# One bank for a block's own keys in the row maxima of a causal attention

## The chip, the core and the metric

The kernel runs on one core of a Trainium2 chip. The metric is the device time of one launch in microseconds (us). A profiled execution comes with it: its span runs from the first to the last instruction, and a little time lies around the span.

The engines are named as the profile names them: PE is the matrix engine (PEld its weight loads, which overlap its products), DVE the vector engine, ACT the scalar engine, POOL the general one, SP the one that issues the DMAs here. PE's results go to PSUM, in banks of 512 fp32 columns by 128 partitions.

## The reference

Four layers follow each other on x (4 batches, 1024 rows, 256 features) with a context of 77 rows a batch. The change is in layer 0, a causal self-attention that also sees the context, then a feed-forward part:

```python
q, k_self, v_self = ...            # 16 heads of 16
k = jnp.concatenate([k_self, k_ctx], axis=1)
scores = jnp.einsum('bthd,bshd->bhts', q, k) * scale
mask = (j >= t) | (j <= i)         # context keys always, own keys up to the row
attn = jax.nn.softmax(jnp.where(mask, scores, -jnp.inf), axis=-1)
x = x + attn @ v
x = x + gelu(ln(ln(x)) @ w1 + b1) @ w2 + b2
```

Layer 1 joins a linear attention to the context with a window attention of 64 rows; layers 2 and 3 are attentions to the context alone.

## The kernel before

**Units.** Layer 0 goes over units: a batch and a block of four heads ("quad"), 16 units in all. A unit's queries and keys lie transposed in one tile, each head in its own 32 partitions, so that the products of the four heads run in four row groups of PE side by side. The keys are ordered with the 77 of the context first, then the 1024 of the sequence: query tile t (128 rows, t = 0 to 7) sees columns 0 to 77 + 128 t + 128, and of the last 128 of them, its own keys, only the lower triangle. Tiles 0 to 3 are block 0, tiles 4 to 7 block 1.

**Two passes.** First the row maxima of the scores are taken (class `Max0`, line 562): queries stand, keys stream, DVE reduces the bank in PSUM to one value for each row and head (line 601), into `mpart`, which has three places for each query tile, head and block. When a block is complete, one small reduce over the places gives the negated maximum (line 609), which PE transposes and DVE adds into a spare row of the queries (`maxima_into`, line 521). Then the scores are computed once more, transposed, keys standing (`Sum0`, line 630); ACT takes the exponential out of PSUM (line 666), and PE multiplies it with the values (`sums`).

**The causal mask.** In the maxima's pass the mask is a product: the identity (bf16) stands, a tile `maskd` with 0 and -1e30 streams, and the product is added into the bank behind the keys' products (lines 587 to 592). `maskd` is made by POOL at the start (lines 205, 227, 228) and is two query tiles wide. A bank that ends one query tile's keys gets 128 columns of it, a bank that ends two gets 256, which are put where the own keys lie.

**Banks and plan.** A bank holds up to 512 columns of scores of a head; `MAX0` (line 620) is the plan written out by hand: eleven banks for a unit, each a list of (query tile, place in `mpart`, first key, last key). The fifth closes block 0, the eleventh block 1.

**Bursts.** `step` (line 485) pairs the eleven banks of a unit with the twelve banks of weights of the unit before (`weights0`; block 0 first). Each pair gives two bursts: two heads of the one beside the other two heads of the other. `burst` (line 471) writes the products in rounds: the maxima's first product for both heads, the weights' first for both heads, the maxima's second, and so on; behind the burst come the reduce and the exponential. A burst takes two buffers of two banks each from a pool of two such buffers (`pair_tile`, line 482), so that its products wait until DVE and ACT have read the burst before. Whichever of the two is taken first goes to the maxima. A PE product in fp32 stands in the profile as two passes, each with its weight load.

**Filler.** Between the bursts `step` puts the weighted sums of the bank before last (only behind the second burst of a pair) and pieces of jobs: projections, feed-forward, preparation of the later layers (`gap`, line 455). A burst's share of the jobs is worked out from the widest bank in it (`cols`). The order of every engine's instructions is thus fixed in the program.

Of the kernel before, what the change touches and what calls it, by code (L numbers as in the profile page):

```python
# [12 lines left out]
BF16 = mybir.dt.bfloat16  # L13
AF = mybir.ActivationFunctionType
ALU = mybir.AluOpType
AX = mybir.AxisListType

P = 128
NB, T, D, S = 4, 1024, 256, 77
# [12 lines left out]
def tile_xattn_seq(ctx: ExitStack, tc: tile.TileContext, d: dict, out: bass.AP):  # L32
    nc = tc.nc
# [5 lines left out]
    work = first.enter_context(tc.tile_pool(name="work", bufs=2))  # L39
# [99 lines left out]
    def clear(qk):  # L139
        nc.gpsimd.memset(qk, 0.0)  # L140
        nc.scalar.activation(qk[:, 1, :], qk[:, 1, :], AF.Identity, bias=onecol, scale=1.0)
# [60 lines left out]


    identb = cpool.tile([P, P], BF16, name="identb")
    maskd = work.tile([P, 2, P], BF16, name="maskd", tag="maskd", bufs=1)
    maskw = work.tile([P, 2, P + WIN], BF16, name="maskw", tag="maskw", bufs=1)
    maskw2 = work.tile([P, 2, P + WIN], BF16, name="maskw2", tag="maskw2", bufs=1)

# [7 lines left out]
    mpart = [work.tile([P, 4, 4, 3], F32, name=f"mpart{i}", tag=f"mpart{i}", bufs=1) for i in range(2)]  # L216
# [4 lines left out]
    def first_constants():  # L221
        clear(qks[0])
        for m in mpart:
            nc.gpsimd.memset(m, NEG)
        nc.gpsimd.tensor_copy(identb, ident)

        nc.gpsimd.memset(maskd, 0.0)
        nc.gpsimd.affine_select(
            out=maskd, in_=maskd, compare_op=ALU.is_ge, fill=NEG, base=0,
            pattern=[[0, 2], [-1, P]], channel_multiplier=1,  # L230
        )
        for m in mrow:
            nc.gpsimd.memset(m, 0.0)
        for v in (vas[0], vcs[0], vas[1], vcs[1]):
            nc.gpsimd.memset(v, 1.0)
# [197 lines left out]
    def defer(gaps, fn):  # L433
        later.append([gaps, fn])

    class Job:


        def __init__(self, gen, n, a=0.0, b=1.0, rest=False):
            self.gen, self.n, self.a, self.b, self.did, self.rest = gen, n, a, b, 0, rest  # L440
# [77 lines left out]
    def rows_of(j):  # L518
        return slice(HP * j, HP * j + HP)

    def maxima_into(qT, q0, m):

        pm = sm.tile([P, 4, P], F32, name="pm", tag="sm")
        for i in range(4):
            nc.tensor.transpose(pm[:, i, :], m[:, i, :], ident)  # L525
        qs = qT[:, q0 : q0 + 512]
        nc.vector.tensor_tensor(qs, pm.rearrange("p i n -> p (i n)"), qs, ALU.add)  # L527

    def extra_of(m):

        return m.rearrange("p i (j r) -> p i j r", r=HP)[:, :, :, DH]
# [30 lines left out]
    class Max0:  # L562

        def __init__(self, u, segs, last):
            self.u, self.segs, self.last = u, segs, last
            self.cols = sum(k1 - k0 for _, _, k0, k1 in segs)

        def matmuls(self, p, ps):  # L570
            u = self.u
            heads = tuple(enumerate((2 * p, 2 * p + 1)))
            rounds, ends, o = [], [], 0
            for t, _, k0, k1 in self.segs:
                qs = slice(P * t, P * t + P)
                rounds.append([
                    ((ps[:, i, o : o + k1 - k0], u["qT"][rows_of(j), qs],
                      u["kT"][rows_of(j), k0:k1]), dict(start=(o == 0), stop=True))
                    for i, j in heads
                ])  # L580
                o += k1 - k0
                if k1 == S + P * t + P:
                    ends.append(o)
            if ends:

                n = len(ends)
                far = ends[-1] - ends[0] if n > 1 else P
                a = ends[0] - P
                rounds.append([
                    ((ps[:, i, a : a + n * far].rearrange("p (k n) -> p k n", k=n)[:, :, 0:P],  # L590
                      identb, maskd[:, 0:n]), dict(start=False, stop=True))
                    for i in range(2)
                ])
            return rounds

        def take(self, p, ps):
            o = 0
            for t, ci, k0, k1 in self.segs:
                bl, i = divmod(t, 4)
                w = k1 - k0  # L600
                nc.vector.tensor_reduce(  # L601
                    mpart[bl][:, i, 2 * p : 2 * p + 2, ci], ps[:, :, o : o + w],
                    axis=AX.X, op=ALU.max,
                )
                o += w
            if self.last is not None and p:
                u, bl = self.u, self.last
                m = mrow[bl]
                nc.vector.tensor_reduce(
                    extra_of(m), mpart[bl], axis=AX.X, op=ALU.max, negate=True  # L610
                )

                def into():
                    maxima_into(u["qT"], 512 * bl, m)
                    u["maxed"].add(bl)

                defer(1, into)


    MAX0 = (  # L620
# [4 lines left out]
    )  # L625

    def maxima0(u):
        return [Max0(u, segs, {4: 0, 10: 1}.get(i)) for i, segs in enumerate(MAX0)]

# [992 lines left out]

    run(stats0(0))
    first_constants()
    head_masks()
    next(keep("c00", lambda: context0(0)))
# [5 lines left out]
    for b in range(NB):  # L1632
        for quad in range(4):
# [12 lines left out]
            u = units[0, b, quad]  # L1646
# [3 lines left out]
    for b in range(NB):  # L1650
        for quad in range(4):
            u = units[1, b, quad]
# [96 lines left out]
```

## Time and profile before

| | us |
|---|---|
| median of 3 runs (2474.48 to 2475.53) | 2475.52 |
| profiled execution | 2472.59 |
| its span | 2470.9 |
| layer 0, paired units, about 112 to 1200 us of the span: PE busy | 988.07 of 1088 |
| in the same stretch: DVE, ACT, POOL busy | 593.14, 440.44, 178.56 |
| all products of layer 0's and 1's scores on PE (`ps<-qk`, with some mask products) | 616.5, 5760 records |
| reduces of the maxima on DVE (line 601), 448 | 409.0 |
| exponentials of layer 0 on ACT (line 666), 384 | 363.2 |

The granted clock of PE is 0.97 of full in layer 0 and 0.99 behind it. In the rows of the profile, L45 is the line of the helper that writes every product, so products are told apart by their tiles: `ps<-qk` are keys' products, `ps<-maskd,identb` the mask. "32x461 f32" is the moving operand, 32 partitions by 461 columns; a merged row names one of the shapes in it.

### The profile page before, as it was taken

To read this page: it belongs to the slowest core of one execution; us is meant where nothing else is said; L and a number is where in the kernel's file an instruction comes from. 1 tells how busy PE (TensorE), PEld (TensorE's weight loads), DVE (VectorE), ACT (ScalarE), POOL (GpSimd) and SP (SyncE) were. 2 spreads that over 40 slices of the span, in tenths; PEclk is the share of its full clock that TensorE was granted. 3 is DMA by queue.
4 is the path that set the end of the run, shared out by engine and by line. 5 is a ranking of instruction groups with operands and counts; after the bars stand their busy time and mean duration, and the time that the engine had idled before them with its cause. 6 is when DMAs were issued, how large, how long until landed. Compare 5 with 4: busy or idle time off the path is not lost.

```text
span 2470.9 us, 39772 instructions
## 1 busy us (share of the span) xinstructions
PE 2284.0 (92%) x16162; PEld 1376.6 (56%) x16162; DVE 1398.5 (57%) x2347; ACT 1033.3 (42%) x1716; POOL 640.5 (26%) x923
## 2 busy tenths in 40 slices
PE   5789989898998989989999999999997999899999
PEld 3433434344444544445456766666654777788887
DVE  4446456654466444665436345454436899776664
ACT  1244344344344334433453343444444677532222
POOL 2011013111131111311134223333341366643222
PEclk9699999999999999999999999999998999999999
DMA  6402021100000000010000100111104334022200
GB/s 176 115 25 93 6 72 41 45 6 14 1 6 15 6 14 2 5 35 5 14 6 14 19 16 15 19 19 19 19 1 151 124 120 133 28 52 57 54 14 18
DMA packets 87136, 98.49 MB, mean 40 GB/s; under 512 B 31222, under 2 KB 77866, under 8 KB 86826
## 3 DMA queue, kind: packets, MB, share of 16 engines
q1 hardware_dynamic: 86954, 95.95, 14.5%
q8 instruction: 128, 2.10, 0.4%
q14 instruction: 54, 0.44, 0.1%
HBM read 57.70 MB, written 20.59 MB: 32 GB/s over the span
## 4 chain that ended last, share of the span: by engine, by line
PE 78%; DVE 11%; ACT 6%; issue 2%; POOL 1%; DMA 1%; SPq 1%; ACTq 0%; DVEq 0%; POOLq 0%
PE ps L45 33%; PE po L45 15%; PE pp L45 6%; PE pv L45 5%; DVE mpart L601 5%; PE ph L45 4%; PE ppv L45 2%; PE psT L1285 2%; PE pvw L45 2%; ACT pe L666 2%; PE ptx L338 1%; PE pvl L45 1%; PE pk L45 1%; PE pt L542 1%; PE pm L525 1%
## 5 line engine op out<-in xcount | busy, mean ns | idle before, releaser
L45 PE MATMUL ps<-qk 32*128 32x192 f32 (+8 forms) x5760 | 616.5, 468 | 102.1 <-DVE mpart L601 54.4
L666 ACT ACTIVATE pe<-ps 128x1024 f32<-128x1024 f32 (+2 forms) x384 | 363.2, 952 | 612.2 <-PE ps L45 607.0
L601 DVE TENSOR_REDUCE mpart<-ps 128x2 f32<-128x1024 f32 (+3 forms) x448 | 409.0, 933 | 349.1 <-PE ps L45 348.7
L45 PEld LDWEIGHTS ps<-qk 32*128 32x128 f32 (+1 forms) x5760 | 288.2, 185 | 375.0 <-DVE mpart L601 134.1
L45 PE MATMUL po<-U,pT 128*128 128x256 f32 (+1 forms) x1280 | 290.5, 382 | 7.4 <-DVE x L1405 4.7
L45 PEld LDWEIGHTS po<-U,pT 128*128 128x128 f32 (+1 forms) x1280 | 239.8, 191 | 50.0 <-ACT pT L1286 8.0
L669 POOL TENSOR_SCALAR_AFFINE_SELECT pe<-pe 128x256 f32<-128x256 f32 (+1 forms) x192 | 95.0, 495 | 637.0 <-ACT pe L666 636.1
L1056 DVE TENSOR_REDUCE mrow<-ps 128x4 f32<-128x768 f32 x128 | 122.5, 957 | 141.4 <-PE ps L45 141.0
L1286 ACT COPY pT<-psT 128x512 f32<-128x512 f32 (+1 forms) x192 | 92.0, 517 | 228.1 <-PE psT L1285 228.0
L1131 ACT ACTIVATE pew<-ps 128x768 f32<-128x768 f32 x128 | 103.4, 811 | 173.4 <-PE ps L45 172.6
L1136 POOL TENSOR_SCALAR_AFFINE_SELECT pew<-pew 128x512 f32<-128x512 f32 x128 | 81.6, 637 | 342.0 <-ACT pew L1131 342.0
L45 PE MATMUL pv<-pe,va 128*32 128x512 f32 (+3 forms) x1536 | 165.0, 518 | 0.1
L45 PE MATMUL ps<-G,xT 128*128 128x308 f32 x512 | 143.0, 423 | 0.0
L45 PE MATMUL ph<-yT,w 128*128 128x256 f32 x512 | 138.1, 405 | 0.8 <-DVE qk L527 0.8
L1366 ACT ACTIVATE s<-s,nm 128x77 f32<-128x77 f32 x512 | 131.2, 352 | 15.9 <-DVE nm L1399 15.9
L1498 POOL TENSOR_TENSOR s<-s,den 128x1232 f32<-128x1232 f32 x32 | 72.0, 2249 | 207.7 <-DVE den L1497 192.4
L45 PEld LDWEIGHTS ph<-yT,w 128*128 128x128 f32 x512 | 93.6, 198 | 52.6 <-issue 39.1
L45 PE MATMUL po<-w,hT 128*128 128x256 f32 x512 | 117.0, 382 | 0.0
L45 PEld LDWEIGHTS ps<-G,xT 128*128 128x128 f32 x512 | 92.4, 190 | 26.8
L45 PEld LDWEIGHTS po<-w,hT 128*128 128x128 f32 x512 | 95.4, 190 | 21.0 <-issue 9.1
L527 DVE TENSOR_TENSOR qk<-pm,qk 128x512 f32<-128x512 f32 x64 | 44.0, 688 | 105.2 <-PE pm L525 105.2
L818 DVE TENSOR_SCALAR hT<-ph,c_L_xattn_b 128x256 f32<-128x256 f32 x128 | 61.3, 480 | 72.4 <-PE ph L45 65.2
(191 smaller groups left out, 3175.7 us busy)
## 6 DMA issues: line engine op xcount, KB each, us to landing
side<-in_fside_t SPq DMA_DIRECT2D x32, 616.0 KB
qk<-st SPq DMA_DIRECT2D x256, 64.0 KB
U<-kept_u SPq DMA_DIRECT2D x8, 1152.0 KB
side<-in_mask_t SPq DMA_DIRECT2D x32, 154.0 KB
G<-kept_g SPq DMA_DIRECT2D x4, 1232.0 KB
x<-in_x SPq DMA_DIRECT2D x8, 512.0 KB
out<-x SPq DMA_DIRECT2D x32, 128.0 KB
kept_u<-st SPq DMA_DIRECT2D x21, 154.0 KB
```

The lines of the kernel that those rows point to most:

```text
L45: nc.tensor.matmul(o, lhsT, rhs, start=start, stop=stop, **kw)
L601: nc.vector.tensor_reduce(mpart[bl][:, i, 2 * p : 2 * p + 2, ci], ps[:, :, o : o + w], axis=AX.X, op=ALU.max,)
L666: nc.scalar.activation(pp[:n, :, o:512], ps[:n, :, o:512], AF.Exp, scale=SC)
L669: nc.gpsimd.affine_select(out=own, in_=own, compare_op=ALU.is_ge, fill=0.0, base=0, pattern=[[0, 2], [0, k], [1, P]], channel_multiplier=-1,)
L818: nc.vector.tensor_scalar(h[:, f, :], ph, cols["L0_xattn_b1"][:, 4 * half + f : 4 * half + f + 1], None, ALU.add,)
L1056: nc.vector.tensor_reduce(mo, ps.rearrange("p j (i n) -> p j i n", i=2)[:, :, :, 0 : P + WIN], axis=AX.X, op=ALU.max, negate=True,)
L1131: nc.scalar.activation(pp[:, :, :, 0 : P + WIN], ps.rearrange("p j (i n) -> p j i n", i=2)[:, :, :, 0 : P + WIN], AF.Exp, scale=SC,)
L1136: nc.gpsimd.affine_select(out=pf[:, :, 0:P], in_=pf[:, :, 0:P], compare_op=ALU.is_ge, fill=0.0, base=0, pattern=[[0, 4], [1, P]], channel_ ...
L1285: nc.tensor.transpose(ps[:, k, :], s[:, P * c : P * c + P], ident)
L1286: nc.scalar.copy(pT[:, 4 * group : 4 * group + n, :], ps[:, 0:n, :])
L1366: nc.scalar.activation(hs, hs, AF.Exp, bias=p1["nm"][:, h : h + 1], scale=SC)
L1498: nc.gpsimd.tensor_tensor(s3, s3, den.unsqueeze(2).to_broadcast([P, H, S]), ALU.mult)
```

## The change

The own keys of the four query tiles of a block are put together in one bank: four products of 128 columns a head, one behind the other, and over them one mask product of 512 columns. `maskd` becomes four query tiles wide. There are two such banks in a unit, named 0 and 1 in the plan, the second and the seventh. The keys in front of the own ones fill the nine other banks, which have no mask any more. The own bank is reduced by one instruction for its four query tiles, into place 0 of `mpart`.

```diff
-    maskd = work.tile([P, 2, P], BF16, name="maskd", tag="maskd", bufs=1)
+    maskd = work.tile([P, 4, P], BF16, name="maskd", tag="maskd", bufs=1)
...
-            pattern=[[0, 2], [-1, P]], channel_multiplier=1,
+            pattern=[[0, 4], [-1, P]], channel_multiplier=1,
...
         def __init__(self, u, segs, last):
-            self.u, self.segs, self.last = u, segs, last
-            self.cols = sum(k1 - k0 for _, _, k0, k1 in segs)
+            self.u, self.segs, self.last, self.own = u, segs, last, None
+            if isinstance(segs, int):
+                self.own = segs
+                self.segs = [
+                    (t, 0, S + P * t, S + P * t + P) for t in range(4 * segs, 4 * segs + 4)
+                ]
+            self.cols = sum(k1 - k0 for _, _, k0, k1 in self.segs)
...
-                if k1 == S + P * t + P:
-                    ends.append(o)
-            if ends:
-
-                n = len(ends)
-                far = ends[-1] - ends[0] if n > 1 else P
-                a = ends[0] - P
+            if self.own is not None:
                 rounds.append([
-                    ((ps[:, i, a : a + n * far].rearrange("p (k n) -> p k n", k=n)[:, :, 0:P],
-                      identb, maskd[:, 0:n]), dict(start=False, stop=True))
+                    ((ps[:, i], identb, maskd.rearrange("p k n -> p (k n)")),
+                     dict(start=False, stop=True))
                     for i in range(2)
                 ])
...
         def take(self, p, ps):
             o = 0
-            for t, ci, k0, k1 in self.segs:
+            if self.own is not None:
+                nc.vector.tensor_reduce(
+                    mpart[self.own][:, :, 2 * p : 2 * p + 2, 0].rearrange("p t j -> p j t"),
+                    ps.rearrange("p j (t n) -> p j t n", n=P), axis=AX.X, op=ALU.max,
+                )
+            for t, ci, k0, k1 in self.segs if self.own is None else ():
...
     MAX0 = (
-        ((3, 0, 0, 461),), ((2, 0, 0, 461),), ((1, 0, 0, 333), (7, 2, 973, 1101)),
-        ((0, 0, 0, 205), (4, 1, 512, 717)), ((5, 1, 512, 845), (3, 1, 461, 589)),
-        ((6, 1, 461, 973),), ((7, 0, 0, 461),), ((7, 1, 461, 973),), ((5, 0, 0, 512),),
-        ((4, 0, 0, 512),), ((6, 0, 0, 461),),
+        ((3, 1, 0, 461),), 0, ((2, 1, 0, 333), (0, 1, 0, 77)), ((6, 1, 512, 845), (4, 1, 512, 589)),
+        ((1, 1, 0, 205), (5, 1, 512, 717)), ((7, 1, 512, 973),), 1, ((7, 2, 0, 512),),
+        ((5, 2, 0, 512),), ((4, 2, 0, 512),), ((6, 2, 0, 512),),
     )
```

In the compiled program the keys' products of the maxima go from 56 to 80 a unit, the mask products from 20 to 8, and the reduces stay at 28.

More of the change, by code (lines that the diff above doesn't have):

```diff
@@ L572, in matmuls @@
             heads = tuple(enumerate((2 * p, 2 * p + 1)))
-            rounds, ends, o = [], [], 0
+            rounds, o = [], 0
             for t, _, k0, k1 in self.segs:
```

## The prediction, made before the changed kernel ran

> **What bounds the kernel now.** I read the page first, for the share of the engines and the chain that ended last; then the stages, by windows; then, inside layer 0, what PE waits for; last the timeline of PE, burst by burst, because the change only reshapes bursts.
>
> ```profile
> span 2470.9 us, 39772 instructions
> ...
> PE 2284.0 (92%) x16162; PEld 1376.6 (56%) x16162; DVE 1398.5 (57%) x2347; ACT 1033.3 (42%) x1716; POOL 640.5 (26%) x923
> ...
> PE 78%; DVE 11%; ACT 6%; issue 2%; POOL 1%; DMA 1%; SPq 1%; ACTq 0%; DVEq 0%; POOLq 0%
> ```
>
> PE carries 78% of the chain and is busy 92%. The windows and PE's waits inside layer 0 say the same of the stage that is changed:
>
> ```profile
> 112.00:1200.00 1088.00, 988.07 (x6964) 464.47 (x6956) 593.14 (x981) 440.44 (x510) 178.56 (x298) 0.97 0.09 24
> ```
>
> ```profile
> PE ps L45 <- DVE mpart L601: 53.1, 80, 1.3
> ...
> PE ps L45 <- ACT pe L666: 15.1, 26, 0.9
> ```
>
> Between 112 and 1200 us PE works 988 of 1088 us; what it does wait for is mostly the reduce of the maxima, whose bank the next burst needs. So time taken from PE's bursts comes back nearly one to one, and the same holds where the reduce is the gate, because the mask stands ahead of the reduce. The masks themselves, shapes kept apart:
>
> ```profile
> L45 PE MATMUL ps<-maskd,identb 128*128 128x256 bf16 x192 | 37.7, 281 | 0.0
> L45 PE MATMUL ps<-maskd,identb 128*128 128x128 bf16 x128 | 18.5, 231 | 0.0
> ```
>
> That is 56 us for all 320, the most that could be at stake. Now the timeline of PE. Its second column is the length of a merged row; the step from one row's start to the next one's is what a piece costs.
>
> ```profile
> 569.62 1.14 PE L45 MATMUL ps<-qk 32*128 32x512 f32 x8
> 570.69 1.98 PE L45 MATMUL pp<-xT,wqk 128*128 128x512 f32 x4
> ```
>
> ```profile
> 612.03 1.37 PE L45 MATMUL ps<-qk 32*128 32x461 f32 x8 [0.52 <-ACT pe L666]
> 613.34 0.29 PE L45 MATMUL ps<-maskd,identb 128*128 128x128 bf16 x2
> 613.55 1.06 PE L45 MATMUL pv<-pe,vc 77*32 77x512 f32 x8
> 614.55 1.42 PE L45 MATMUL ps<-qk 32*128 32x333 f32 x16
> 615.90 0.39 PE L45 MATMUL ps<-maskd,identb 128*128 128x256 bf16 x2
> ```
>
> ```profile
> 1200.55 1.10 PE L45 MATMUL ps<-qk 32*128 32x64 f32 x16
> 1201.58 0.50 PE L45 MATMUL ps<-maskw,identb 128*128 128x384 bf16 x2
> ...
> 1508.43 0.50 PE L45 MATMUL ps<-maskw,identb 128*128 128x384 bf16 x2
> 1508.86 1.06 PE L45 MATMUL pvl<-pel,vc 77*32 77x512 f32 x8
> ```
>
> To be seen: a burst of four 512-column products, each in its own 32 rows and each recorded as two passes, takes 1.07 us. The pair of masks adds 0.21 us at 128 columns (613.34 to 613.55) and 0.43 at 384 (1508.43 to 1508.86) when a product in 32-column tiles follows; at 256 columns with a full-array product behind, 0.23 (the next row starts at 616.13). So a pair costs 0.107 us per 128 columns plus a fixed part: about 0.10 us before a tiled product, about 0.015 before a full-array one. That fixed part, not the columns, is what the change can save.
>
> **The masks.** A unit is one block of four heads; there are 16, and units 1 to 15 pair each bank of maxima with a bank of weights. For each pair of heads the old plan has masks over 1, 2, 2, 2 and 1 own tiles in five bursts, eight tiles in all; the new has four and four in two bursts, also eight. The columns cancel. Three pairs go per head pair, two head pairs, 15 units: 90 pairs. In the second burst of a bank the weighted sums, tiled, always follow: 45 x 0.10 = 4.5 to 4.9 us. In the first burst comes filler: of the 45 old 256-column pairs there the timeline shows 27 followed by a full-array product, 8 by a tiled one, 10 by PE waiting. For these last the reduce starts 0.62 us after the burst's last pass starts when there is no mask, 0.84 with 128 columns: the fixed part is 0.22 - 0.107 = 0.115. So 27 x 0.015 + 18 x 0.11 = 2.4 us. Together -7.0 us; the ends are -5.2 (all first bursts at 0.015) and -9.9 (all at 0.11).
>
> **The own banks.** Instead of one product of 461 or 512 columns a head they run four of 128, each with two passes and its own weight load, while the weights' 512 columns run in the other two row groups. That is 24 products and 48 loads more a unit. The columns are no more than before, so the question is whether loads keep up. The trace's single records give it: in the burst at 1200.55 (64, 128 and 192 columns in turn beside 512) the loads of one row group start 109, 112, 112 and 111 ns apart, and a 128-column pass after a 333-column one (614.55) follows the former pass by 112 ns. 128 columns of a pass take 107 ns ((384 - 104)/333 = 0.84 ns a column, 104 ns until the first pass streams). So eight passes: 104 + 107 + 6 x 112 + 107 + 88 ns of ending = 1.08 us against 1.07: +0.013 us x 60 bursts = +0.8 us.
>
> [...] In the burst at 1200.55 the 128-column pass, issued behind the 512-column product, starts at 0.271, before that product's second pass at 0.505, and the burst takes 1.03 us to the mask (1201.58). [...]
>
> If the 512-column product of the burst has to wait for its bank (ACT or DVE), the own tiles behind it wait as well. They then need 6 x 112 + 195 ns = 0.87 us, less than the 1.02 of the product they stand behind: nothing is added.
>
> **The other key bursts.** 333 + 77 in place of 333 + 128 beside 384 + 128: 1.095 becomes about 1.08 (without a mask the nearest row, 461 beside 384 + 128, takes 1.08), -0.015 x 30 = -0.5 us. 205 + 205 beside 256 becomes 333 + 77 beside 256, and 333 + 128 beside 512 becomes 205 + 205 beside 512: in most of them the second product waits for its bank 0.3 to 0.5 us, then runs its own 0.65 or 1.02 us; the same before and after, 0. The rest are 512 beside 512 or less.
>
> **DVE, ACT, POOL, SP.** Still 14 reduces a head pair, over the same columns (a reduce costs 1224 ns at 1024 elements, 852 at 666, 416 at 256: near enough a line), so 0; five bursts change by about 0.1 us up or down and cancel. The bank of own keys is reduced in one instruction of the 1024-element size. The last bank of each block stays in its place (fifth and eleventh), so the transposition of the maxima and the weights behind it keep their turn. The due times of the filler follow each burst's widest bank, 512 or 410 as before, so no job, no DMA on SP and no eviction is moved in units 1 to 15. Building the wider mask on POOL costs some 0.3 us at 16 us (0.31 + 0.42 us now), while the first burst runs at 39.9 us: hidden by 20 us and more. Unit 0 has no weights beside it: three groups of four masks fewer at about 0.1 us, eight more loads a burst: 0.
>
> Sum: -7.0 + 0.8 - 0.5 = -6.7 us. The profiled execution was 2472.6 us (span 2470.9 and 1.7 around it), 2.9 below the median of the runs; the same 6.7 off the median 2475.5 gives 2468.8, say 2469.
>
> **Rivals.** (a) The reduce is the gate almost everywhere, so each lost pair frees 0.115: -10.4, 2464 to 2465. For it speak 53 us of waits for the reduce, against it that PE idles only some 9% of the layer. [...] (c) Slower: loads throttle the own banks. In the three-tile burst one 128-column pass follows another by 165 ns (0.271 to 0.436), though the loads were 112 apart. If all six spacings were 165, an own burst would last 1.40 us: +0.325 x 60 = 19.5, less 7.5, is +12: 2487. It breaks even at about 132 ns and is slower by over 5 us from 145.
>
> **Numbers.** A measurement of this kernel can tell about 0.2%, 5 us, from no change. The forecast, 2465.5 to 2473, has 0.50; (a) 0.12; (b) 0.22; (c) 0.16. Faster by over 5 us: 0.35 of the forecast and all of (a), 0.47. Slower: (c) and a little of (b), 0.18. The rest, 0.35, within. Range: from the full mask bound less the second-order gain, 2462, to just short of (c)'s whole price, 2484.
>
> **What would show it.** 128 mask products of 512 columns in place of 320, a pair taking 0.44 us before full-array and 0.54 before tiled products; own bursts of 1.08 us before their mask (1.26: program order holds; 1.4: loads); reduce time of the maxima the same; PE idle in layer 0 near 100 us as before. I am wrong if the own bursts exceed 1.2 us, or if PE's wait for DVE or ACT grows by what its busy time loses.

## The result and the profile after

| | before | after |
|---|---|---|
| median of 7 runs (lowest to highest), us | 2474.01 (2471.02 to 2475.53) | 2466.58 (2463.03 to 2472.39) |
| profiled execution; its span, us | 2472.59; 2470.9 | 2470.36; 2468.7 |

The ratio after to before is 0.9973, with 95% interval 0.9962 to 0.9985. The forecast was 2469.0, range 2462 to 2484. What follows shows that the number is nearer the mark than its terms: of the 7.4 us between these medians the step-for-step comparison below gives about 3 to the change.

Page and window of the changed kernel:

```profile
span 2468.7 us, 40924 instructions
...
PE 2273.2 (92%) x16738; PEld 1410.7 (57%) x16738; DVE 1399.1 (57%) x2347; ACT 1032.1 (42%) x1716; POOL 640.1 (26%) x923
...
PE 77%; DVE 11%; ACT 6%; issue 2%; POOL 1%; DMA 1%; SPq 1%; ACTq 0%; DVEq 0%; POOLq 0%
```

```profile
112.00:1200.00 1088.00, 978.54 (x7575) 499.34 (x7572) 598.80 (x989) 443.38 (x516) 178.88 (x299) 0.97 0.10 24
```

PE's busy time in layer 0 went from 988.07 to 978.54 us, 9.5 less, while the span lost only 2.2. PE's waits from 112 to 1190 us say where some of it went:

```profile
PE ps L45 <- DVE mpart L606: 54.2, 83, 1.3
PE ps L45 <- ACT pe L671: 22.1, 30, 1.6
...
PE ps L45 <- DVE mpart L599: 2.8, 14, 0.2
```

Lines 606 and 599 are the reduces (599 that of the own bank), 671 the exponential. The wait for DVE went from 53.1 to 54.2 + 2.8, that for ACT from 15.1 to 22.1: together 11 us more of waiting (9.5 in the second profiles of both kernels, 70.0 and 79.5). That is one of the two marks named beforehand for being wrong: the wait grew by about what busy time lost.

The bursts themselves are as forecast. Groups by shape, and PE's timeline:

```profile
L606 DVE TENSOR_REDUCE mpart<-ps 128x2 f32<-128x1024 f32 x128 | 156.3, 1224 | 102.2 <-PE ps L45 102.1
L599 DVE TENSOR_REDUCE mpart<-ps 128x8 f32<-128x1024 f32 x64 | 78.2, 1225 | 84.9 <-PE ps L45 84.9
...
L606 DVE TENSOR_REDUCE mpart<-ps 128x2 f32<-128x922 f32 x64 | 71.5, 1119 | 76.7 <-PE ps L45 76.7
...
L45 PE MATMUL ps<-maskd,identb 128*128 128x512 bf16 x128 | 40.5, 403 | 0.0
```

```profile
640.78 1.16 PE L45 MATMUL ps<-qk 32*128 32x128 f32 x20
641.87 0.61 PE L45 MATMUL ps<-maskd,identb 128*128 128x512 bf16 x2
642.41 1.07 PE L45 MATMUL pv<-pe,va 128*32 128x512 f32 x8
...
676.96 1.16 PE L45 MATMUL ps<-qk 32*128 32x128 f32 x20 [0.62 <-DVE mpart L606]
678.05 0.61 PE L45 MATMUL ps<-maskd,identb 128*128 128x512 bf16 x2
678.50 0.60 PE L542 MATMUL pt<-ident,sT 128*128 128x128 f32 x4
```

An own burst (x20: four products of each of two heads in two passes, and two heads' weights) takes 1.09 us to its mask (640.78 to 641.87, 676.96 to 678.05): 1.08 was forecast, with 1.26 and 1.40 as the marks of a wrong one. The pair of masks takes 0.54 us before a tiled product and 0.45 before a full-array one, as forecast (0.54 and 0.44). The reduce over four query tiles costs what the plain one costs, 1225 against 1224 ns.

### The profile page after: what moved, and what is told of

Same layout as the page of the kernel before. It is cut to its first block, busy times and chain, and to the rows that moved or that the text cites. A ratio compares the mean times of both kernels' runs of the same rounds, so it can differ in the third digit from the quotient of the medians.

```text
span 2468.7 us, 40924 instructions
## 1 busy us (share of the span) xinstructions
PE 2273.2 (92%) x16738; PEld 1410.7 (57%) x16738; DVE 1399.1 (57%) x2347; ACT 1032.1 (42%) x1716; POOL 640.1 (26%) x923
## 4 chain that ended last, share of the span: by engine, by line
PE 77%; DVE 11%; ACT 6%; issue 2%; POOL 1%; DMA 1%; SPq 1%; ACTq 0%; DVEq 0%; POOLq 0%
PE ps L45 33%; PE po L45 15%; PE pp L45 6%; DVE mpart L606 5%; PE pv L45 5%; PE ph L45 4%; PE ppv L45 2%; PE psT L1290 2%; PE pvw L45 2%; ACT pe L671 2%; PE ptx L338 1%; PE pvl L45 1%; PE pt L542 1%; PE pm L525 1%; PE pk L45 1%
## 5 line engine op out<-in xcount | busy, mean ns | idle before, releaser
L45 PE MATMUL ps<-qk 32*128 32x192 f32 (+9 forms) x6528 | 611.8, 435 | 113.1 <-DVE mpart L606 54.4
L45 PEld LDWEIGHTS ps<-qk 32*128 32x128 f32 (+1 forms) x6528 | 329.8, 187 | 381.4 <-issue 125.7
L606 DVE TENSOR_REDUCE mpart<-ps 128x2 f32<-128x1024 f32 (+4 forms) x384 | 331.0, 885 | 268.2 <-PE ps L45 267.9
L674 POOL TENSOR_SCALAR_AFFINE_SELECT pe<-pe 128x256 f32<-128x256 f32 (+1 forms) x192 | 94.7, 494 | 636.1 <-ACT pe L671 635.1
L599 DVE TENSOR_REDUCE mpart<-ps 128x8 f32<-128x1024 f32 x64 | 78.2, 1225 | 84.9 <-PE ps L45 84.9
```

What stands on the lines that cost most here:

```text
L45: nc.tensor.matmul(o, lhsT, rhs, start=start, stop=stop, **kw)
L599: nc.vector.tensor_reduce(mpart[self.own][:, :, 2 * p : 2 * p + 2, 0].rearrange("p t j -> p j t"), ps.rearrange("p j (t n) -> p j t n", n= ...
L606: nc.vector.tensor_reduce(mpart[bl][:, i, 2 * p : 2 * p + 2, ci], ps[:, :, o : o + w], axis=AX.X, op=ALU.max,)
L674: nc.gpsimd.affine_select(out=own, in_=own, compare_op=ALU.is_ge, fill=0.0, base=0, pattern=[[0, 2], [0, k], [1, P]], channel_multiplier=-1,)
```

## What repeats in a profile, and what does not

The 95% interval of the first comparison did not hold up in longer ones: unaltered copies of the changed kernel gave 0.9994 and 0.9998. So the small effects below are read in another way, from one trace each.

PE's clock has only two values in the records of the two profiles, 1.0 and 0.5 of full. The half-clock stretches within the span last 3.41 us or multiples of it, up to 20.48, and fall at other places from one execution to the next (between 400 and 700 us at 436.6, 453.7, 467.3, 580.0, 641.4 and 665.3 before, at 451.8, 465.4, 499.6 and 636.1 after). They make up the 0.97 of layer 0: 75 of its 1088 us run at half before, 56 after, which takes off 0.035 and 0.026. I cut layer 0 at the end of each burst's last reduce, which gives 22 steps a unit, took units 1 to 15, left out the steps that come within 1 us of a half-clock stretch in either trace, and compared like with like: the mean difference of a step times 15. Some 88% of the steps are left. Two profiles of the same kernel then agree in the sum within 0.3 us (kernel before: +0.3; changed kernel: -0.2), where the same steps with the stretches in them differ by -11.8 and +1.9 us. I call this the clean sum. From before to after it is -3.48; with the second profile of the changed kernel -3.60; from the second profile of before to the third of the changed kernel -3.57.

This is the clean difference bank by bank, in ns for the first and second burst of each bank; worked out from the traces, with the plan's own part beside it (that is, both kernels without their masks, as measured below):

```
bank        before -> after     without masks     columns, before -> after
1st           -94    +21          -87     -1       461 -> 461
2nd (own)    +446   +305         +331   +110       461 -> 512
3rd          -636   -335         -330    -49       461 -> 410
4th           -21   -148          +69    +12       410 -> 410
5th          -367   -326          -91    -84       461 -> 410
6th          -407   -320          -84   -151       512 -> 461
7th (own)    +992   +528         +527   +100       461 -> 512
8th          -343   +115         -344    +99       512 -> 512
9th, 10th       0      0            0      0       512 -> 512
11th         +194   +163         +192   +164       461 -> 512
sum x 15          -3.5 us             +5.7 us
```

## The experiments

Each ratio is to the kernel before, run beside it on the same chip. Clean sums are against the second profile of the changed kernel, unless another kernel is named.

**The changed kernel once more**, unaltered, for a second profile and for longer timing.

> The changed kernel once more, unaltered, to narrow the interval and to have a second profile. Theory A (what is saved is the fixed part of 90 mask pairs, some 7 us, and it appears in layer 0 alone): ratio 0.997, the stretch from the first reduce of the second unit to the last unit of layer 0 shorter by about 7 us, the start and the later layers the same. Theory B (the gain is larger in layer 0, because the third to fifth bank's bursts no longer have a mask, and part of it is given back in waits of the own banks and at the start): layer 0 shorter by about 12 us as in the first profile, 2 us lost before the second unit again.

Measured: 2469.54 us against 2474.40, 0.9994 [0.998, 1.0008]. The clean sum repeats to 0.2 us and is neither the 7 nor the 12 us of the two theories. The size of the first comparison does not repeat.

**The masks alone, in the old plan and in the new.** Both kernels leave out the mask in the maxima's pass, so the value subtracted in the exponent is the maximum over the whole own tile; the mask of the weights stays.

```diff
-            if ends:
+            if ends and False:
```

> The kernel before with the mask products of layer 0's maxima left out, so that each row's maximum runs over all 128 own keys of its tile; the weights come out the same, as the same value is taken from numerator and sum. Theory A: all mask time lies on the path. 150 pairs cost 2.46 us a unit by the steps of the trace (first bursts 2 x 0.124 + 3 x 0.27, second bursts 2 x 0.216 + 3 x 0.324), 37 us in 15 units and 2 in the first: -39 us, about 2435. Rival (masks are partly hidden behind PE's waits for ACT, whose exponential starts before the mask): -20 to -28 us.

```diff
-            if self.own is not None:
+            if self.own is not None and False:
                 rounds.append([
```

> The changed kernel with the mask products of layer 0's maxima left out, same remark on the maxima as for the kernel before without them. Theory A: 60 pairs of 0.44 and 0.54 us: -30 us against the changed kernel; so -37 against the kernel before, and within 3 us of the kernel before without masks, because the banks without their masks are worth the same in both plans. Theory B (the plan of the banks gains on its own): faster than the kernel before without masks by 5 us or more. Theory C (own banks cost, the third to fifth bank only gained as their masks went): slower than the kernel before without masks by 5 us or more.

Measured: 2431.06 (0.9825 [0.9806, 0.9844]) and 2441.28 (0.9872 [0.9853, 0.9891]). By clean sums, each against its own kernel, the old masks cost 34.6 us and the new ones 25.5 (421 and 327 ns a burst in the 2nd bank, 419 and 386 in the 7th). So the same mask columns cost 9.1 us less in two bursts of a head pair than in five. (The exponential, which the rival has ahead of the mask, starts on the median 0.13 us behind the first mask product in the trace of the kernel before.) And without any mask the new plan is slower than the old by 5.7 us, as theory C had it: the regrouping of the banks costs most of what the masks save. (The medians of these few runs lie 10.2 us apart, but at mean granted clocks of 0.973 and 0.971.) PE's waits alone do not show why. First the old plan without masks, then the new:

```profile
PE ps L45 <- DVE mpart L601: 70.0, 112, 1.4
...
PE ps L45 <- ACT pe L666: 15.4, 22, 1.2
```

```profile
PE ps L45 <- DVE mpart L606: 54.6, 84, 1.3
PE ps L45 <- ACT pe L671: 29.3, 35, 1.6
```

The new plan waits for ACT twice as long, but for DVE less by as much: the two make 85.4 and 83.9 us. In the clean steps PE's wait for DVE falls by 14.8 us, that for ACT grows by 13.2, and PE's busy time grows by 6.3. So the loss stands in PE's busy time and not in the sum of its waits; what lengthens the busy time is not shown. The table puts the excess in the 2nd, 7th and 11th bank, which grew, against too small a return in the others.

**The four own products first.** A burst with an own bank issues its eight own products before the weights' ones.

```diff
+        first = parts[0][0]
+        if getattr(first, "own", None) is not None and parts[1][0] is not first:
+            m, t = rows
+            rows = [[sum(m[:-1], []), m[-1]], [sum(t, [])]]
```

> The changed kernel with all four own products of a head written ahead of the weights' product in the burst, the mask behind both. In the changed kernel the second to fourth own product stand behind the weights' product, and PE sits idle 0.6 us in a number of bursts while that one waits for its bank. Theory A (each row group takes its products on its own as far as the queue goes, since own passes overtook a second pass of the 512-column product): the weights' product starts at once beside the own ones when nothing waits, bursts stay at 1.09 us, and where its bank is late the own ones are done meanwhile: -3 to -10 us against the changed kernel. Rival (PE takes its instructions in order; the loads of the fourth own product hold up what stands behind them): the weights' product starts 0.7 to 0.8 us late, an own burst takes 1.8 to 1.9 us, 60 bursts lengthen by up to 0.75: +20 to +45 us.

Measured: 2504.67, 1.0115 [1.0091, 1.0139]; clean +22.8 us. The timeline:

```profile
703.30 1.69 PE L45 MATMUL ps<-qk 32*128 32x128 f32 x20
704.92 0.61 PE L45 MATMUL ps<-maskd,identb 128*128 128x512 bf16 x2
```

The own burst takes 1.62 us to its mask in place of 1.09. In its single records the weights' product starts 0.56 us late (703.861), with the first pass of the third own product. So products written in front of it hold it up, although they use other rows of PE; but it does not wait for all of them, as it starts 0.21 us ahead of the fourth own product (704.072), which is written in front of it too. What sets the 0.56 us no run shows. The order that the change has, weights' product as the second of the round, is worth 528 ns in the first bursts of both own banks, 338 and 121 on the mean in the second ones.

**One product in place of four.** Own bank of one 512-column product a head; mask and reduce as they are, so three tiles' maxima are taken over other rows' scores.

```diff
-            for t, _, k0, k1 in self.segs:
+            segs = self.segs
+            if self.own is not None:
+                t = 4 * self.own
+                segs = [(t, 0, S + P * t, S + P * t + 512)]
+            for t, _, k0, k1 in segs:
```

> The changed kernel with each own bank made by one product of 512 columns a head (the first query tile of the block against all own keys of the block) in place of four of 128; mask, reduce and everything else stay. The maxima of the other three query tiles are then not those of the reference, and neither is the output; only the time is looked at. Outside the stretches at half clock, cycle by cycle against the changed kernel, in the 15 paired units: theory H (the second to fourth own product stand behind the weights' product, which waits for its bank; this is what the new plan without masks pays against the old one without masks, 5.7 us): -4 to -8 us, seen in the second and seventh bank. Rival W (what is paid is the width: three banks grow from 461 to 512 columns where the reduce is the gate, and those that shrink lie where ACT or filler is): 0 to -1.5 us.

Measured: 2468.50, 0.9983 [0.9971, 0.9994]; clean -0.93 us, 5 to 19 ns in each own burst. So the four products cost 0.8 to 0.9 us. No more than that of the plan's 5.7 lies in them, or in own tiles that stand behind a waiting weights' product: theory H fell.

**Eight mask products of 128 columns in place of two of 512.**

```diff
-                    ((ps[:, i], identb, maskd.rearrange("p k n -> p (k n)")),
+                    ((ps[:, i, P * k : P * k + P], identb, maskd[:, k]),
                      dict(start=False, stop=True))
-                    for i in range(2)
+                    for i in range(2) for k in range(4)
```

> The changed kernel with the mask of an own bank written as four products of 128 columns a head in place of one of 512; the columns and the places stay, 12 products more a burst group of two heads become 6 more. Cycle by cycle against the changed kernel: if the fixed part of a mask lies with the pair (going from row groups to the full array and back), the columns alone count, 0 to +1 us; if with the product, 6 x 0.05 us x 60 bursts = +18 us; if the identity's weight load sets the pace of a 128-column product (some 0.09 us a product by the first unit's groups of four, at a partly halved clock), 8 x 0.09 in place of 0.44: +0.28 x 60 = +17 us.

```profile
685.28 1.16 PE L45 MATMUL ps<-qk 32*128 32x128 f32 x20
686.37 0.62 PE L45 MATMUL ps<-maskd,identb 128*128 128x128 bf16 x8
686.92 1.07 PE L45 MATMUL pv<-pe,vc 77*32 77x512 f32 x8
```

Measured: 2470.71, 0.9994 [0.9981, 1.0007]; clean +1.1 us. The group takes 0.55 us (686.37 to 686.92) in place of 0.54: six more products cost 15 to 28 ns. The fixed part of a mask pair is thus not a price per product: it is paid once for the group. In the rows before the change it is 0.10 us where a tiled product follows (613.34 to 613.55, less 0.107 for the columns) and 0.015 where a full-array one does (615.90 to 616.13, less 0.215); what it is paid for no run shows.

**The 6th bank and the 11th change their widths.**

```diff
-        ((1, 1, 0, 205), (5, 1, 512, 717)), ((7, 1, 512, 973),), 1, ((7, 2, 0, 512),),
-        ((5, 2, 0, 512),), ((4, 2, 0, 512),), ((6, 2, 0, 512),),
+        ((1, 1, 0, 205), (5, 1, 512, 717)), ((6, 2, 0, 512),), 1, ((7, 2, 0, 512),),
+        ((5, 2, 0, 512),), ((4, 2, 0, 512),), ((7, 1, 512, 973),),
```

> The changed kernel with the sixth and the eleventh bank exchanged: 512 columns of query tile 6 in the sixth, the 461 of query tile 7 in the eleventh. Work and instruction counts stay. Theory W (a bank's width costs where the reduce is the gate, 0.19 us a burst for 51 columns in the eleventh, and less in the sixth): eleventh -0.36, sixth +0.24 us a unit, -1 to -3 us in 15 units. Rival (a width costs the same everywhere): 0.

Measured: 2470.04, 0.9982 [0.9967, 0.9996]; clean -0.2 us. The 6th rose by 192 and 143 ns, the 11th fell by 191 and 163, the 1st and 7th took up the rest (+95, -81). So 51 columns have the same price at these two places, 0.14 to 0.19 us a burst where the table's two bursts gave 0.08 and 0.15 for the 6th. My theory that the 11th is a worse place fell. The size is that of PE and DVE together: two passes of 51 columns at 0.84 ns are 86 ns, and the reduce over 102 elements more takes 105 to 107 ns (1224 less 1119 for 1024 against 922).

**A better packing for the plan without masks**: the old plan, masks left out as above, tiles put together otherwise so that the wide banks stand beside the wide weights' banks.

```diff
-            if ends:
+            if ends and False:
...
-        ((3, 0, 0, 461),), ((2, 0, 0, 461),), ((1, 0, 0, 333), (7, 2, 973, 1101)),
-        ((0, 0, 0, 205), (4, 1, 512, 717)), ((5, 1, 512, 845), (3, 1, 461, 589)),
-        ((6, 1, 461, 973),), ((7, 0, 0, 461),), ((7, 1, 461, 973),), ((5, 0, 0, 512),),
-        ((4, 0, 0, 512),), ((6, 0, 0, 461),),
+        ((3, 0, 0, 512),), ((2, 0, 0, 461),),
+        ((1, 0, 0, 333), (3, 1, 512, 589), (7, 2, 1024, 1101)),
+        ((0, 0, 0, 205), (4, 2, 666, 717)), ((5, 0, 0, 512),), ((6, 0, 0, 512),),
+        ((5, 1, 512, 845), (4, 1, 512, 666)), ((7, 0, 0, 512),), ((7, 1, 512, 1024),),
+        ((4, 0, 0, 512),), ((6, 1, 512, 973),),
```

> The old class without masks and with a plan made for that: the own keys need no place of their own, so the bank that stands beside the weights' bank of 256 columns (the fourth) gets only 256, the rest fills banks of 461 to 512, one reduce more a pair of heads. Maxima over all own keys of a tile as in the other kernels without masks; the weights come out the same. Against the old plan without masks: the fourth bank's bursts go from 0.94 to 1.07 down to 0.66 us, -0.3 to -0.4 x 30 = -9 to -12, some of it paid back by the wider banks beside reduces: -5 to -9 us, so about 2424. Rival (DVE and ACT are the gate in these short bursts): 0 to -2 us.

Measured: 2431.36, 0.9829 [0.9814, 0.9844], no gain over 2431.06, where 5 to 9 us were expected; units 1 to 15 take 1044.1 us of its trace against 1041.1, stretches included. Why it gains nothing is not shown: the plan also changes the fourth bank's share of the filler, which follows the widest bank of a burst.

**Both kernels once more**, to time an unaltered copy of each against the kernel before.

> The kernel before against itself, for the size of what chance does. Theory K (outside the stretches in which PE is granted half its clock, an execution repeats to the nanosecond; what differs from run to run is how many such stretches fall into it): cycle by cycle between the two profiles of the kernel before, under 0.5 us over 15 units outside the stretches; time against granted clock on one line, some 1.6 us for 0.001; ratio 1.000, but single medians up to 5 us apart. Rival (the spread comes from transfers or waits): cycles differ by microseconds outside the stretches too.

> The changed kernel a third time, beside the kernel before on the same chip. Theory K: the change is worth -3.5 us at full clock, as the cycles outside the half-clock stretches say, so the ratio tends to 0.9985, and to 0.997 or 1.000 as the half-clock stretches fall. Rival (the first result is the size): 0.997.

Measured: 2475.08, 1.0012 [0.9994, 1.0029], and 2470.39, 0.9998 [0.9983, 1.0014]. Copies of one kernel come out 0.1% apart, and the change is hardly more than that.

**The narrowed banks widened by 51 columns.** Third bank, then fifth, both in the changed kernel:

```diff
-        ((3, 1, 0, 461),), 0, ((2, 1, 0, 333), (0, 1, 0, 77)), ((6, 1, 512, 845), (4, 1, 512, 589)),
+        ((3, 1, 0, 461),), 0, ((2, 1, 0, 384), (0, 1, 0, 77)), ((6, 1, 512, 845), (4, 1, 512, 589)),
```

> The changed kernel with 51 columns more in the third bank (query tile 2 against 384 keys in place of 333; the added ones are own keys, whose maxima may only raise the value that is subtracted). Theory W (the price of columns depends on the place: where PE waits for the reduce, a burst pays product and reduce of them, 0.19 us): +0.38 us a unit, the size by which this bank got cheaper in the new plan without masks: +5.7 us in 15 units outside the half-clock stretches. Rival (columns beside a weights' bank of 512 are hidden): 0.

```diff
-        ((1, 1, 0, 205), (5, 1, 512, 717)), ((7, 1, 512, 973),), 1, ((7, 2, 0, 512),),
+        ((1, 1, 0, 205), (5, 1, 512, 768)), ((7, 1, 512, 973),), 1, ((7, 2, 0, 512),),
```

> The changed kernel with 51 columns more in the fifth bank (query tile 5 against 256 keys in place of 205, same remark as for the third). Theory W: here PE waits for ACT (some 0.5 us in the first burst), so the columns cost less: 0.175 us a unit as in the new plan without masks, +2.6 us in 15 units. Rival (51 columns cost the same at every place): +5.7 us as in the third.

Measured: 2474.63 (1.0013 [0.9997, 1.0029]) and 2469.92 (0.9994 [0.9984, 1.0004]); clean +3.6 and +1.6 us. In the third bank 51 columns cost 151 and 112 ns, with 32 returned in the fourth; in the fifth 105 and 91, of which the sixth's first burst returns 106 at once. The order is the one that the theory of unequal prices gave, the sizes are two thirds of it; an equal price, or one that lies only in the fifth, is excluded.

## Why the prediction came out

**Masks: right in kind, too small.** -7.0 us was forecast with ends -5.2 and -9.9; the two kernels without masks give 25.5 - 34.6 = -9.1. The term that was too small is not the lost pairs' fixed part. The pairs as PE's timeline has them are 2.46 us a unit before (from the expectation of the old kernel without masks), 36.9 in 15 units, and 30 x (0.44 + 0.54) = 29.4 after: 7.5 us apart, near the forecast. Taken out, both sets are worth less than that, the old by 2.3 us, the new by 3.9. The forecast counted every pair as wholly on the path; that the masks that stay are hidden more than those that went is the other 1.6. (Of the 45 first-burst pairs the trace has 28 before full-array products, 8 before tiled ones and 9 before waits, not 27, 8 and 10; this is worth 0.1 us.)

**Own banks: right.** +0.8 forecast, +0.9 measured by one product in place of four. Loads do not throttle here (1.09 us a burst, not 1.40), and the three further tiles, also behind a waiting product, add 5 to 19 ns a burst. The mark of 1.26 us for program order rests on no run; what the runs show is an order neither strict nor free. In the burst at 640.78 us an own pass starts 0.325 us in, before the second pass of the weights' product in front of it at 0.547. With all own products first the weights' product waits 0.56 us, yet starts before the last of them. And in the changed kernel's burst at 154.62 us, where the weights' product starts only at 0.695, once DVE has read its bank, the next own product behind it starts at 0.708.

**The other banks: wrong.** This is the step "five bursts change by about 0.1 us up or down and cancel", with "-0.5" for the other key bursts. The plan alone cost 5.7 us, so 4.8 remain beside the own products' 0.9. The columns do cancel, 51 up in three banks and 51 down in three. Their price doesn't. By the column without masks the 2nd bank took 0.44 us a unit more, the 7th and 8th 0.38, the 11th 0.36, in all 1.18. The third and fourth returned 0.30, the fifth 0.18, the sixth 0.24, the first 0.09, in all 0.80. The widened fifth bank shows one place of it: there 51 columns are worth 0.10 us a unit, while in the third they are worth 0.23, since the burst behind the fifth gives half of it back. Why the 2nd costs 0.08 us a unit more than the 11th, and both more than the third or the fifth, no run separates; the four products, with 0.02 to 0.03 us a unit in each own bank, are not it.

**POOL: wrong by 0.4 us.** "Hidden by 20 us and more" looked only at who reads the mask. It stands in POOL's queue ahead of other constants, and DVE waits for one of those. Before, DVE's row was:

```profile
21.31 0.16 DVE L248 TENSOR_REDUCE hsel<-hsel 128x2 f32<-128x8 f32 x1 [9.30 <-POOL hsel L244]
```

After, POOL's rows, then DVE's:

```profile
17.12 0.52 POOL L227 MEMSET maskd<- 128x512 bf16 x1
17.71 0.64 POOL L228 TENSOR_SCALAR_AFFINE_SELECT maskd<-maskd 128x512 bf16<-128x512 bf16 x1
...
22.32 0.19 POOL L244 TENSOR_SCALAR_AFFINE_SELECT hsel<-hsel 128x8 f32<-128x8 f32 x1
```

```profile
22.55 0.16 DVE L248 TENSOR_REDUCE hsel<-hsel 128x2 f32<-128x8 f32 x1 [9.73 <-POOL hsel L244]
22.92 5.59 DVE L317 TENSOR_SCALAR xn<-x,mv,rs 128x256 f32<-128x256 f32 x4
```

The wait is 9.29 or 9.30 us in four profiles with the small mask, 9.73 or 9.74 in four with the wide one. Behind it on DVE stands the normalization that PE's first transposes wait for, so 0.43 us go onto its start. How much of it lasts is not shown: half-clock stretches lie over unit 0, which ends at 111.5 to 113.2 us in four profiles with the small mask and at 109.8 to 113.6 in ten with the wide one.

**The sum.** -9.1 + 0.9 + 4.8 + 0.4 = about -3.0, where -6.7 was forecast. (The first three terms close a ring of four kernels, so that they meet the clean sum of -3.5 is no proof of their own.) The runs set the size less firmly. 41 of the changed kernel average 2469.96 us, 134 of the kernel before 2472.34 (one run of 2892 left out), a difference of -2.4 with an interval of 1.3 either way from their spread. But the time follows the granted clock: over 108 runs of the kernel before it falls by about 1.6 us for each 0.001 (fitted 2472.9 at 0.970, 2469.6 at 0.972), and the changed kernel's runs had 0.9712 on the mean against 0.9703. At the same clock, with one slope for both kernels, the difference is only -0.8, 0.6 either way. Whether the change brings the higher clock or chance does, and why this lies under the 3.0 of the traces, no run shows.

The forecast's time was met by luck. The first seven runs of the changed kernel had granted clocks of 0.970 to 0.976, 0.973 on the mean. And over all runs two errors cancel: the base of 2475.5 was some 3 us above what the kernel before averages, and the gain was forecast some 4 us too large. The second mark for being wrong, that PE's waits for DVE or ACT grow by what its busy time loses, told the mechanism best: in the clean steps PE's busy time falls by 8.9 us, and its waits for ACT and DVE grow by 5.3 and 2.1. The 0.22 of (b) stood for little left of the gain, which is what came. Rivals (a) and (c) are out.

## What to carry to other kernels

Columns moved from one bank to another cancel on paper only: price each burst by what ends last there. Here 51 columns were worth between 0.10 and 0.44 us a unit, by their place. A constant made early on a busy queue costs whoever waits for anything behind it, not only its readers: here DVE's wait for POOL went from 9.30 to 9.73 us. And ask first whether a step is needed at all: softmax needs an upper shift for each row and not the exact maximum, so the old plan without the maxima's mask, at 2431 us (0.9825), beats both kernels, as long as a masked score isn't so far above the row's own that its exponentials vanish.

## What the runs showed of the hardware

Outside the half-clock stretches most steps repeat to 1 to 3 ns between executions (sums over 15 units to 0.3 us, with the stretches in them only to 11.8); the spread of the runs (2458 to 2480 us for the kernel before, granted clock 0.979 to 0.965) goes with the granted clock, at a correlation of -0.93 over the 127 whose clock is on record. Six more mask products cost 15 to 28 ns in all (685.28 us in the run with masks by tile), while a pair's fixed part is about 0.1 us between tiled products (613.34 to 613.55 before the change, less 0.107): the group pays, not the product. Products in different rows of PE can start out of their written order (0.325 against 0.547 us in the changed kernel, 703.861 against 704.072 with own products first), but a product with many others in front of it does wait (0.56 us there).
